# Two transformer layers with routed experts on one core: keys and values from combined weights, a choice of experts on logits, and a written-out end of layer 1

## The chip, the core and the metric

The kernel runs on one core of a Trainium2 chip. A core has separate engines that each work through their own queue of instructions: PE (TensorE, matrix products), DVE (VectorE), ACT (ScalarE), POOL (GpSimd) and SP (SyncE, which here only starts transfers). They wait for one another by semaphores. The metric is the device time of one execution in microseconds (us), and the median of the runs is what is compared. A traced execution gives the time of every instruction; the trace's span runs from its first to its last recorded event.

## The reference

The input is `x` of 8 x 1024 tokens of 128 numbers. All is float32. Four blocks follow, each added to its input, each behind a layer norm:

```python
# layer 0, attention: 8 heads of 32, keys and values through 64 numbers
q = (x @ Wq.T).reshape(b, t, 8, 32)
kv_latent = x @ Wkv_down.T                      # [64]
k = (kv_latent @ Wk_up.T).reshape(b, t, 8, 32)
v = (kv_latent @ Wv_up.T).reshape(b, t, 8, 32)
attn = softmax(einsum('bqhd,bkhd->bhqk', q, k) * 32 ** -0.5)
out = einsum('bhqk,bkhd->bqhd', attn, v).reshape(b, t, 256) @ Wo.T
# layer 0, experts: 2 of 14, F = 256
probs = softmax(x @ gate_w.T)
top2_p, top2_i = top_k(probs, 2)
w = top2_p / maximum(top2_p.sum(-1), 1e-10)
... = w[:, 0] * expert(top2_i[:, 0]) + w[:, 1] * expert(top2_i[:, 1])
# layer 1, linear attention: 16 heads of 8, running sums over the sequence
out = q @ cumsum(k v) / (q @ cumsum(k) + 1e-6) @ Wo.T
# layer 1, experts: 1 of 8, F = 512; above 1280 tokens an expert
# keeps the likeliest, the others go to expert 0
final_e = route(tokens, router_w)
y = relu(tokens @ W1[e] + b1[e]) @ W2[e] + b2[e]
```

## The kernel before

**Attention of layer 0.** Work goes by blocks: one group of four heads and 512 queries. A block has 16 steps (`HALVES`), and the variable `h` counts the steps of all 32 blocks. In a step, `scores` (L398) makes scores of 128 keys against 512 queries for two heads, with ACT's exponential. `smax_step` (L634) makes the largest scores of a block that lies `LEAD` = 24 steps ahead, `weigh` (L413) multiplies earlier exponentials by values (`num`) or by ones (`den`), and POOL adds exponentials in pairs so that `den` needs half the products. The instructions of PE, DVE and ACT go out in the order in which the code writes them (a manual schedule). For POOL and SP, `pinned` calls keep their order.

Other work is put between the steps by hand: `at(h, f)` puts a piece into step `h`. `prepare(b)` (L692) does so with what batch `b` needs in its 64 steps: layer norm, transposes, two `latent` steps (L327, 64 numbers for each token), `project` (L346) for queries and keys, `values` (L335). For batch 0 this is done ahead of the first step (L640 to L658). `complete(b)` (L708) places what follows a batch: output projection, layer norm, and the eleven pieces of `Finish.choice` (L619), the choice of two experts. `last_half` does so for half of batch 7, and the other half comes behind the last block (L790 to L816). In the last 24 steps nothing lies ahead; the code calls them quiet, and there DVE makes the pair sums.

`Finish.choice` makes logits (PE), the maximum and differences (DVE), exponentials (ACT), sum, reciprocal and product (DVE); then twice a maximum, an equality, an index (`candidates`, `choose`). `count` and `rank` give every token its place in its expert's region of the DRAM table `rows_in`, `places` (L593) turns this into addresses. `moving` collects scatters: indirect transfers, issued by POOL, of one row for each of 128 tokens. In the attention loop one goes out every fourth step, in the quiet steps one each step.

**Experts of layer 0.** `expert_tables` (L149) makes, from the counts of tokens per expert, two tables for the tiles of 256 rows: where a tile starts (`row_j`) and which expert it has (`exp_j`). SP reads `row_j` value by value (L200) to fetch tiles; each is transposed, multiplied by two weight matrices and written to `rows_out`.

**Layer 1.** Its loop (L1468) runs over `t`, the pairs of 128-token groups: 32 pairs, four per batch, and three more turns to empty the pipeline. A turn works on several pairs at different stages: gathers of the experts' rows (POOL), `combine` and `stats` for pair t+3, projections for t+1, scores for t, `within` and `turned` for t-1, `project_out` for t-2, and `offset`, `back_norm`, `back_transposed` (layer norm ahead of the experts) for t-3. `stats` (L1026) ends with a power on POOL (`rs`). POOL's gathers, powers and scatters stand in one queue. Two scatters of an earlier batch's rows go out per turn. The pieces of `Route` (L1286), the choice of one expert, are put into slots of later turns by `planned` (L1426). Batch 7 is routed in two halves of four groups: the first from turn 32, the second in turn 34. A `Route` is made like a choice of layer 0, with one expert.

**Experts of layer 1.** `expert_tables` again makes the table, in a pool `d_tab`, then `tiles1` (L1518) runs 36 tiles; SP fetches them from the DRAM table `rows1`, and POOL writes finished rows to `out`. Further tiles and `dropped` run only where experts are overfull.

Of the kernel before, what the change touches and what calls it, by code (L numbers as in the profile page):

```python
# [16 lines left out]
P = 128  # L17
NB = 8
# [34 lines left out]
NOT_AN_EXPERT = 1000.0  # L53
# [24 lines left out]
def tile_two_layers(  # L78
# [36 lines left out]
    def probabilities(b, w_sb, ne, psum, ptag):  # L115

        lg = psum.tile([P, CPB, ne], F32, name="lg", tag=ptag)
        for c in range(CPB):
            nc.tensor.matmul(
                lg[:, c, :], lhsT=xT[b][:, c * P:(c + 1) * P], rhs=w_sb, start=True, stop=True  # L120
            )
        shape = [P, CPB, ne]
        mx = stat.tile([P, CPB], F32, name="mx")
        nc.vector.tensor_reduce(mx, lg, AX.X, ALU.max)
        pr = stat.tile(shape, F32, name="pr", tag=f"pr{ne}")
        nc.vector.tensor_tensor(pr, lg, mx.unsqueeze(2).to_broadcast(shape), ALU.subtract)
        nc.scalar.activation(pr, pr, AF.Exp)
        sm = stat.tile([P, CPB], F32, name="sm")
        nc.vector.tensor_reduce(sm, pr, AX.X, ALU.add)
        nc.vector.reciprocal(sm, sm)  # L130
        nc.vector.tensor_tensor(pr, pr, sm.unsqueeze(2).to_broadcast(shape), ALU.mult)
        return pr

    def first_of_largest(pr, ne, indices, oh, fi):


        shape = [P, CPB, ne]
        pm = stat.tile([P, CPB], F32, name="pm")
        nc.vector.tensor_reduce(pm, pr, AX.X, ALU.max)
        cand = stat.tile(shape, F32, name="cand", tag=f"cand{ne}")  # L140
        nc.vector.tensor_tensor(cand, pr, pm.unsqueeze(2).to_broadcast(shape), ALU.is_equal)
        nc.vector.scalar_tensor_tensor(
            cand, cand, -NOT_AN_EXPERT, indices.unsqueeze(1).to_broadcast(shape), ALU.mult, ALU.add
        )
        nc.vector.tensor_reduce(fi, cand, AX.X, ALU.min)
        nc.vector.tensor_tensor(oh, cand, fi.unsqueeze(2).to_broadcast(shape), ALU.is_equal)
        return pm

    def expert_tables(tab, psum, ptag, counts, ne, nt):  # L149
# [21 lines left out]
        ej = tab.tile([1, nt], F32, name="ej")  # L171
        nc.vector.tensor_reduce(ej, past, AX.X, ALU.add)
        nc.vector.tensor_scalar(ej, ej, float(ne - 1), None, ALU.min)
        exp_j = tab.tile([1, nt], mybir.dt.int32, name="exp_j")
        nc.vector.tensor_copy(exp_j, ej)
# [8 lines left out]
        nc.vector.tensor_tensor(past, past, hop[0:1].unsqueeze(1).to_broadcast(jshape), ALU.mult)  # L184
        rj = tab.tile([1, nt], F32, name="rj")
        nc.vector.tensor_reduce(rj, past, AX.X, ALU.add)
# [3 lines left out]
        nc.vector.tensor_copy(row_j, rj)  # L190
        return SimpleNamespace(exp_j=exp_j, row_j=row_j, base=base, tot=tot, upto=upto)
# [35 lines left out]
    with ExitStack() as ph:  # L227
# [14 lines left out]
        wkd_sb = wts.tile([P, R0], F32, name="wkd_sb")  # L242
# [12 lines left out]
        nc.gpsimd.memset(ones_h, 1.0)  # L255
        def load_rest():
# [17 lines left out]
        kvls, vs, outs = {}, {}, {}  # L274
# [52 lines left out]
        def latent(b, h):  # L327
            ps = bank(name="lat")
            cols = slice(h * BLK, (h + 1) * BLK)
            if h == 0:  # L330
                kvls[b] = work.tile([R0, T], F32, name="kvl", bufs=1)
            nc.tensor.matmul(ps[:R0, :], lhsT=wkd_sb, rhs=xT[b][:, cols], start=True, stop=True)
            nc.scalar.copy(kvls[b][:, cols], ps[:R0, :])

        def values(b, c2):  # L335
            ps = bank((P, 2, 8 * HD0), "val")
            if c2 == 0:
                vs[b] = work.tile([P, CPB, 8 * HD0], F32, name="v")
            for i in range(2):
                c = 2 * c2 + i  # L340
                nc.tensor.matmul(
                    ps[:, i, :], lhsT=kvls[b][:, c * P:(c + 1) * P], rhs=wvu_sb, start=True, stop=True
                )
            nc.scalar.copy(vs[b][:, 2 * c2:2 * c2 + 2, :], ps)

        def project(n, of_k, h):  # L346

            b, g = divmod(n, 2)
            if n not in kTs:
                qTs[n] = work.tile([P, T], F32, name="qT", bufs=3)  # L350
                kTs[n] = work.tile([P, T], F32, name="kT", bufs=3)
            dst, w, src = (kTs, wku_sb, kvls) if of_k else (qTs, wq_sb, xT)
            cols = slice(h * BLK, (h + 1) * BLK)
            ps = bank(name="prj")
            nc.tensor.matmul(ps, lhsT=w[:, g * P:(g + 1) * P], rhs=src[b][:, cols], start=True, stop=True)
            nc.scalar.copy(dst[n][:, cols], ps)
# [103 lines left out]
        class Finish:  # L460
# [46 lines left out]
            def exponentials(self):  # L507
                nc.scalar.activation(self.pr, self.pr, AF.Exp)

            def softmax(self):  # L510
                sm = self.tile("sm", [P, self.n])
                nc.vector.tensor_reduce(sm, self.pr, AX.X, ALU.add)
                nc.vector.reciprocal(sm, sm)
                nc.vector.tensor_tensor(
                    self.pr, self.pr, sm.unsqueeze(2).to_broadcast(self.shape), ALU.mult
                )

            def candidates(self, pr):
                pm = self.tile("pm", [P, self.n], bufs=4)
                nc.vector.tensor_reduce(pm, pr, AX.X, ALU.max)  # L520
                cand = self.tile("cand")
                nc.vector.tensor_tensor(cand, pr, pm.unsqueeze(2).to_broadcast(self.shape), ALU.is_equal)
                nc.vector.scalar_tensor_tensor(
                    cand, cand, -NOT_AN_EXPERT,
                    cst[:, C_I14:C_I14 + E0].unsqueeze(1).to_broadcast(self.shape), ALU.mult, ALU.add,
                )
                return pm, cand
# [8 lines left out]
            def first(self):  # L536
                self.p1, self.cand = self.candidates(self.pr)

            def second(self):
                self.oh1 = self.choose(0, self.cand)  # L540
                rest = self.tile("rest", bufs=1)
                nc.vector.scalar_tensor_tensor(rest, self.oh1, -2.0, self.pr, ALU.mult, ALU.add)
                self.rest = rest

            def third(self):
                self.p2, self.cand = self.candidates(self.rest)

            def fourth(self):
                self.oh2 = self.choose(1, self.cand)

# [42 lines left out]
            def places(self):  # L593

                n, b, c0 = self.n, self.b, self.c0
                at = stat0.tile([P, 2, CPB], U32, name="at")
                for k in range(2):
# [4 lines left out]
                        to, chosen[:, k, b, c0:c0 + n], float(REG0), mine, ALU.mult, ALU.add  # L602
                    )
                    nc.vector.tensor_scalar(at[:, k, :n], to, float(TW0), None, ALU.add)
                xn = self.xn

                def move(j, k):
                    ins = nc.gpsimd.indirect_dma_start(  # L608
                        out=rows_in, out_offset=bass.IndirectOffsetOnAxis(ap=at[:, k, j:j + 1], axis=0),
# [7 lines left out]
                moving.extend(lambda j=j, k=k: move(j, k) for j in range(n) for k in range(2))  # L617

            def choice(self):  # L619
                return [  # L620
                    self.logits, self.exponentials, self.softmax, self.first, self.second, self.third,
                    self.fourth, self.count, self.rank, self.places, self.weights,
# [19 lines left out]
        norms = [Norm(0, c0, CPK, xn, xT[0]) for c0 in (0, CPK)]  # L642
        for f in norms:
# [7 lines left out]
        for h in range(2):  # L651
            latent(0, h)
# [39 lines left out]
        def prepare(b):  # L692
# [4 lines left out]
            for i, h in enumerate((17, 20)):  # L697
                at(h0 + h, latent, b, i)
            for (of_k, i), h in zip(((True, 0), (False, 0), (True, 1), (False, 1)), (24, 25, 28, 29)):
# [8 lines left out]
        def complete(b):  # L708
# [6 lines left out]
            hs = (36, 37, 38, 42, 46, 50, 54, 58, 60, 62, 66)  # L715
            if b == NB - 2:
                hs = (33, 34, 34, 38, 40, 41, 42, 42, 43, 44, 45)
# [3 lines left out]
        def last_half():  # L721
# [5 lines left out]
            for h, piece in zip((51, 52, 53, 54, 55, 56, 57, 57, 58, 59, 60), f.choice()):  # L727
# [12 lines left out]
        for n, qb in blocks:  # L740
            for kc in range(CPB):
                for hp in range(2):
# [24 lines left out]
                    if kc % 2 == 1 and hp == 1:  # L767
                        for i in range(4):
                            if not quiet:
                                pinned(nc.gpsimd.tensor_tensor, first[:, i, :], first[:, i, :], e[:, i, :], ALU.add)  # L770
                            else:
# [18 lines left out]
        n, qb = blocks[-1]  # L790
        weigh(*weighing, den=False)
        weigh(*summing, den=True)
# [83 lines left out]
    with ExitStack() as ph:  # L876
# [60 lines left out]
        def places():  # L937
# [3 lines left out]
            for b in range(0, NB, NB // 2):  # L941
                for k in range(2):
# [4 lines left out]
                        pick, of_expert, cst[:, C_J:C_J + E0].unsqueeze(1).to_broadcast(shape), ALU.is_equal  # L947
# [55 lines left out]
    with ExitStack() as ph:  # L1003
# [22 lines left out]
        def stats(p):  # L1026
# [10 lines left out]
            tc.keep_in_program_order(nc.gpsimd.tensor_tensor(rs, ve, mhalf[:, :PAIR], ALU.pow))  # L1037
# [16 lines left out]

        products = []

        def behind_within(ins):

            if products:
                tc.add_manual_dep(  # L1060
                    ins, products.pop(),
                    mybir.DependencyInfo(mybir.DependencyClass.Sync, mybir.DependencyReason.DATA),
                    reason="the order of issue",
                )
# [221 lines left out]
        class Route:  # L1286
# [23 lines left out]
            def exponentials(self):  # L1310
                nc.scalar.activation(self.pr, self.pr, AF.Exp)

            def softmax(self):
                sm = self.tile("sm1", [P, self.n])
                nc.vector.tensor_reduce(sm, self.pr, AX.X, ALU.add)
                nc.vector.reciprocal(sm, sm)
                nc.vector.tensor_tensor(
# [497 lines left out]
```

## Time and profile before

| | us |
|---|---|
| median of 3 runs | 2088.29 (2085.06 to 2090.93) |
| the profiled execution | 2075.58 |
| its span | 2073.8 |

The span falls into stages. The table gives the busy time of three engines in each, and the clock that the throttle granted to TensorE as a share of full speed:

| stretch, us | what | PE | DVE | POOL | clock |
|---|---|---|---|---|---|
| 0 to 20 | loading, batch 0 | 9.38 | 3.80 | 5.28 | 1.00 |
| 20 to 1305 | attention, layer 0 | 1269.10 | 935.75 | 820.91 | 0.99 |
| 1305 to 1336 | last choice, table | 5.25 | 17.97 | 13.51 | 0.50 |
| 1336 to 1490 | experts of layer 0 | 153.79 | 100.75 | 48.09 | 0.98 |
| 1490 to 1525 | first gathers | 9.06 | 10.76 | 22.33 | 0.56 |
| 1525 to 1877 | layer 1, full turns | 351.18 | 250.54 | 193.19 | 0.92 |
| 1877 to 1923 | layer 1, last turns, table | 13.24 | 17.97 | 21.73 | 0.61 |
| 1923 to 2074 | experts of layer 1 | 136.79 | 69.79 | 79.33 | 0.95 |

A line of the profile gives the source line, the engine, and the operation with its result and operands by their names in the program (`num<-e,v`), partitions x elements, and then times. "PE L332 MATMUL lat<-xT,wkd_sb" is the latent's product in L332. A line that begins with an engine's name and "q" is that engine's queue control. Matmuls are pipelined: in the timeline a matmul's end is modelled, so the distance from one start to the next is what a step holds PE.

### The profile page before, as it was taken

The page shows a single profiled execution, that of the slowest core. Times are in us where ns is not written, and L with a number is a line of the kernel's source. Part 1 is how long each engine was busy: PE and PEld are TensorE (multiplying, and loading weights), DVE is VectorE, ACT ScalarE, POOL GpSimd, SP SyncE. Part 2 cuts the span into 40 slices and gives each one's busy share as a digit, 9 for nine tenths or more (in the row PEclk, how much of TensorE's full clock was granted, in tenths as well). Part 3 has the DMA queues.
Part 4 walks back from the last instruction along what each step waited for, and adds up shares of the span by engine and source line. Part 5 has one row for each costly group of instructions (what it writes and reads, how often), then busy time and mean ns, then how long its engine had stood idle before and what let it go on. Part 6 is the DMA issues. An engine that isn't in the chain of part 4 may idle for free. (4 is left out here: it accounts for less than half of the span.)

```text
span 2073.8 us, 45378 instructions
## 1 busy us (share of the span) xinstructions
PE 1947.8 (94%) x17426; PEld 1005.2 (48%) x17426; DVE 1407.3 (68%) x3614; ACT 1121.2 (54%) x2356; POOL 1204.4 (58%) x1320
## 2 busy tenths in 40 slices
PE   7999999999999999999999997499779999994997
PEld 3333333333333333333333333399747777773896
DVE  6767768758768768768767776567547787764453
ACT  2655555555565565565565455166447766661443
POOL 1556656657667667667666775423355576634455
PEclk9999999999999999999999999699959999995999
DMA  6000000000000000000000000144323311111331
GB/s 225 1 2 2 1 2 3 8 7 9 8 8 9 8 8 10 8 8 8 9 7 8 15 8 26 46 140 137 101 59 85 94 53 49 48 34 52 105 105 58
DMA packets 49872, 81.58 MB, mean 39 GB/s; under 512 B 13498, under 2 KB 32449, under 8 KB 49521
## 3 DMA queue, kind: packets, MB, share of 16 engines
q0 software_dynamic: 17808, 41.55, 6.1%
q1 hardware_dynamic: 28384, 29.10, 4.9%
q10 hardware_dynamic: 3456, 7.95, 1.2%
q8 instruction: 140, 2.29, 0.5%
q14 instruction: 84, 0.68, 0.1%
HBM read 42.73 MB, written 35.96 MB: 38 GB/s over the span
## 5 line engine op out<-in xcount | busy, mean ns | idle before, releaser
L370 DVE TENSOR_REDUCE nmp<-big 128x1 f32<-128x512 f32 x1000 | 642.0, 682 | 295.3 <-PE st L406 259.3
L409 ACT ACTIVATE e<-st 128x512 f32<-128x512 f32 x1000 | 544.3, 595 | 467.6 <-PE st L406 398.8
L240 POOL TENSOR_TENSOR e<-e 128x512 f32<-128x512 f32 x488 | 603.4, 1265 | 50.0 <-PE num L423 50.0
L366 PE MATMUL big<-kT,qT 32*128 32x512 f32 x2000 | 630.4, 641 | 0.2 <-DVE nmp L370 0.2
L406 PE MATMUL st<-qT,kT 32*128 32x512 f32 x2000 | 530.0, 589 | 0.0
L423 PE MATMUL num<-e,v 128*32 128x512 f32 x3064 | 300.7, 465 | 8.5 <-ACT nums L451 8.5
L240 POOL TENSOR_TENSOR outT<-nums,dens 128x64 f32<-128x64 f32 x248 | 79.1, 320 | 376.4 <-DVE dens L441 275.0
L406 PEld LDWEIGHTS st<-qT,kT 32*128 32x128 f32 x2000 | 212.7, 191 | 2.9 <-issue 1.2
L405 PE MATMUL st<-nb,ones_h 3*128 3x512 bf16 x1000 | 210.5, 385 | 1.3 <-DVE nmp L370 1.3
L405 PEld LDWEIGHTS <-ones_h 3*128 3x128 bf16 x1024 | 51.1, 91 | 320.5 <-issue 314.5
L423 PEld LDWEIGHTS num<-e,v 128*32 128x32 f32 x3064 | 61.3, 108 | 296.9 <-issue 264.6
L366 PEld LDWEIGHTS big<-kT,qT 32*128 32x128 f32 x2000 | 194.6, 183 | 21.9 <-DVE nmp L370 17.9
L1072 POOL DMA_INDIRECT got<-rows_out,found x128 | 126.0, 984 | 97.1 <-PE tp L1107 44.9
L608 POOL DMA_INDIRECT rows_in<-xn,at x128 | 132.1, 1032 | 45.2 <-issue 32.8
L441 DVE RECIPROCAL dens<-dens 128x64 f32<-128x64 f32 x248 | 129.9, 536 | 17.1 <-ACT dens L436 17.0
L423 PE MATMUL den<-e,ones 128*32 128x512 f32 x1024 | 141.0, 608 | 0.2 <-POOL e L240 0.2
L1585 POOL DMA_INDIRECT out_x<-y,to x72 | 79.3, 1102 | 74.7 <-DVE y L1583 58.0
L1566 ACT ACTIVATE g<-ph,wt 128x256 f32<-128x256 f32 x144 | 63.8, 474 | 92.6 <-PE ph L1563 92.6
L933 POOL DMA_DIRECT2D rows_out<-y x77 | 44.5, 578 | 106.9 <-DVE y L932 99.7
L923 PEld LDWEIGHTS py<-wt,g 128*128 128x128 f32 x616 | 80.8, 192 | 3.9
L1037 POOL TENSOR_TENSOR rs<-ve,mhalf 128x2 f32<-128x2 f32 x64 | 46.4, 726 | 62.0 <-DVE ve L1035 53.5
L923 PE MATMUL py<-wt,g 128*128 128x128 f32 x616 | 81.0, 275 | 0.0
(284 smaller groups left out, 2989.1 us busy)
## 6 DMA issues: line engine op xcount, KB each, us to landing
xr<-rows_in SPq DMA_DIRECT2D x77, 128.0 KB
rows_out<-y POOLq DMA_DIRECT2D x77, 128.0 KB, 2.3
xr<-rows SPq DMA_DIRECT2D x36, 257.0 KB
nb<-part SPq DMA_DIRECT2D x384, 1.0 KB
blob<-in_blob ACTq DMA_DIRECT2D x8, 578.0 KB
blob<-in_blob SPq DMA_DIRECT2D x1, 4494.0 KB
x<-in_x SPq DMA_DIRECT2D x8, 512.0 KB
rows<-nil ACTq DMA_DIRECT2D x9, 257.0 KB
```

The costliest lines, as they stand in the source:

```text
L240: return tc.keep_in_program_order(f(*args, **kw))
L366: nc.tensor.matmul(ps, lhsT=qTs[n][r, qc * P:(qc + 1) * P], rhs=kTs[n][r, kb * BLK:(kb + 1) * BLK], start=True, stop=True,)
L370: nc.vector.tensor_reduce(nmps[n][:, h, qc, kb:kb + 1], ps, AX.X, ALU.max, negate=True)
L405: nc.tensor.matmul(st, lhsT=ones_h[r3, :], rhs=nbs[n][r3, cols], start=True, stop=False)
L406: nc.tensor.matmul(st, lhsT=kTs[n][r, kc * P:(kc + 1) * P], rhs=qTs[n][r, cols], start=False, stop=True)
L409: nc.scalar.activation(e[:, h, :], st, AF.Exp, scale=SCALE0)
L423: nc.tensor.matmul(vds[key][32 * h:32 * h + 32, cols], lhsT=ones[:, :HD0] if den else vs[b][:, kc, c0:c0 + HD0], rhs=e[:, h, cols], start= ...
L441: nc.vector.reciprocal(s[:, cols], s[:, cols])
L608: ins = nc.gpsimd.indirect_dma_start(out=rows_in, out_offset=bass.IndirectOffsetOnAxis(ap=at[:, k, j:j + 1], axis=0), in_=xn[:, c0 + j, :] ...
L923: nc.tensor.matmul(ps[:, i, :], lhsT=g[:, k, i * P:(i + 1) * P], rhs=w[:, B_W2 + k * D:B_W2 + (k + 1) * D], start=k == 0, stop=k == K0 - 1,)
L1072: ins = tc.keep_in_program_order(nc.gpsimd.indirect_dma_start(out=gots[p][:, i, k, :], out_offset=None, in_=rows_out, in_offset=bass.Indir ...
L1585: ins = nc.gpsimd.indirect_dma_start(out=out_rows, out_offset=bass.IndirectOffsetOnAxis(ap=at[:, i:i + 1], axis=0), in_=y[:, i, :], in_off ...
```

## The change

The change has these parts.

1. Keys and values of layer 0 come straight from the normalised tokens. Two products at the start (`combined_weights`) multiply the down projection by each up projection, two ACT copies put the results into `wk_sb` and `wv_sb`; `latent` is gone, `project` for keys and `values` contract 128 numbers in place of 64. Their places among the steps move four steps forward in `prepare` for the first head group. `wkd` is loaded in its other orientation.
2. The choice in layer 0 works on logits less their maximum: the largest is where this is 0. `first` follows `logits` at once, the exponential goes into its own tile `ex`, the second choice is made on the differences too, and the softmax is reduced to the two probabilities that are needed (`exponential2`, `softmax`), placed behind `places`. Indices are scaled by 1/`UNIT` so that one operation compares and inserts the index. Each of the two address sets has its own tile, and all scatters of first choices come before those of second choices.
3. In layer 0's last block the last pair sums on DVE are dropped; `den` takes the two tiles one after the other.
4. `expert_tables` makes `row_j` ahead of `exp_j`.
5. `Route` in layer 1 is made in the same way as the choice in layer 0: `choose` needs the differences alone.
6. Two scatters per slot go out in layer 1's turns once the gathers have ended, and five at the end of turn 31. The powers issued then stand behind the scatters before them (`since`, `behind`). The route of batch 6 is a turn earlier.
7. The last three turns of layer 1 are written out in a new order.
8. The pool `d_tab` gets `reuse_waits="tile"`: its tiles wait for what last used their own memory and not for all of the pools before. The table's code is in a manual schedule for PE and DVE.

```diff
-        def latent(b, h):
-            ps = bank(name="lat")
...
-            nc.tensor.matmul(ps[:R0, :], lhsT=wkd_sb, rhs=xT[b][:, cols], start=True, stop=True)
-            nc.scalar.copy(kvls[b][:, cols], ps[:R0, :])
+        def combined_weights():
+            ps = bank((P, 2, 8 * HD0), "lat")
+            for i, w in enumerate((wku_sb, wvu_sb)):
+                nc.tensor.matmul(ps[:, i, :], lhsT=wkd_sb, rhs=w, start=True, stop=True)
+            nc.scalar.copy(wk_sb, ps[:, 0, :])
+            nc.scalar.copy(wv_sb, ps[:, 1, :])
...
-                    ps[:, i, :], lhsT=kvls[b][:, c * P:(c + 1) * P], rhs=wvu_sb, start=True, stop=True
+                    ps[:, i, :], lhsT=xT[b][:, c * P:(c + 1) * P], rhs=wv_sb, start=True, stop=True
...
-            dst, w, src = (kTs, wku_sb, kvls) if of_k else (qTs, wq_sb, xT)
+            dst, w = (kTs, wk_sb) if of_k else (qTs, wq_sb)
...
             def first(self):
-                self.p1, self.cand = self.candidates(self.pr)
+                cand = self.tile("cand")
+                nc.vector.scalar_tensor_tensor(cand, self.pr, 0.0, self.indices(), ALU.is_lt, ALU.max)
+                self.oh1 = self.choose(0, cand)
 
             def second(self):
-                self.oh1 = self.choose(0, self.cand)
                 rest = self.tile("rest", bufs=1)
-                nc.vector.scalar_tensor_tensor(rest, self.oh1, -2.0, self.pr, ALU.mult, ALU.add)
+                nc.vector.scalar_tensor_tensor(rest, self.oh1, -LOW, self.pr, ALU.mult, ALU.add)
+                self.top2 = self.tile("top2", [P, self.n])
+                nc.vector.tensor_reduce(self.top2, rest, AX.X, ALU.max)
                 self.rest = rest
 
             def third(self):
-                self.p2, self.cand = self.candidates(self.rest)
+                cand = self.tile("cand")
+                nc.vector.tensor_tensor(
+                    cand, self.rest, self.top2.unsqueeze(2).to_broadcast(self.shape), ALU.is_lt
+                )
+                nc.vector.tensor_tensor(cand, cand, self.indices(), ALU.max)
+                self.cand = cand
...
+            def exponential2(self):
+                self.e2 = self.tile("e2", [P, self.n])
+                nc.scalar.activation(self.e2, self.top2, AF.Exp)
+
+            def softmax(self):
+                self.p1, self.p2 = (self.tile(name, [P, self.n]) for name in ("p1", "p2"))
+                nc.vector.tensor_reduce(self.p1, self.ex, AX.X, ALU.add)
+                nc.vector.reciprocal(self.p1, self.p1)
+                nc.vector.tensor_tensor(self.p2, self.e2, self.p1, ALU.mult)
...
-                moving.extend(lambda j=j, k=k: move(j, k) for j in range(n) for k in range(2))
+                moving.extend(lambda j=j, k=k: move(j, k) for k in range(2) for j in range(n))
...
                 return [
-                    self.logits, self.exponentials, self.softmax, self.first, self.second, self.third,
-                    self.fourth, self.count, self.rank, self.places, self.weights,
+                    self.logits, self.first, self.exponentials, self.second, self.third, self.fourth,
+                    self.exponential2, self.count, self.rank, self.places, self.softmax, self.weights,
                 ]
...
+        combined_weights()
         for f in norms:
...
-        for h in range(2):
-            latent(0, h)
         for of_k, h in ((False, 0), (True, 0), (True, 1)):
...
-            for i, h in enumerate((17, 20)):
-                at(h0 + h, latent, b, i)
-            for (of_k, i), h in zip(((True, 0), (False, 0), (True, 1), (False, 1)), (24, 25, 28, 29)):
+            for (of_k, i), h in zip(((True, 0), (False, 0), (True, 1), (False, 1)), (20, 21, 24, 25)):
                 at(h0 + h, project, 2 * b, of_k, i)
...
-            hs = (36, 37, 38, 42, 46, 50, 54, 58, 60, 62, 66)
+            hs = (36, 38, 37, 42, 46, 50, 47, 54, 56, 58, 62, 66)
             if b == NB - 2:
-                hs = (33, 34, 34, 38, 40, 41, 42, 42, 43, 44, 45)
+                hs = (33, 34, 34, 38, 39, 40, 40, 41, 42, 43, 44, 45)
...
-                            else:
+                            elif h < STEPS - 1:
                                 nc.vector.tensor_tensor(first[:, i, :], first[:, i, :], e[:, i, :], ALU.add)
...
+        weigh(n, qb, CPB - 2, first, den=True)
+        weigh(*weighing, den=True)
         weigh(*weighing, den=False)
-        weigh(*summing, den=True)
...
-            tc.keep_in_program_order(nc.gpsimd.tensor_tensor(rs, ve, mhalf[:, :PAIR], ALU.pow))
+            ins = tc.keep_in_program_order(nc.gpsimd.tensor_tensor(rs, ve, mhalf[:, :PAIR], ALU.pow)).ins
+            if gathered[0] == PAIR * NPAIR:
+                for name in since:
+                    behind(ins, name)
+            since.clear()
...
+                nc.vector.scalar_tensor_tensor(
+                    cand, self.pr, 0.0, cst[:, C_I8:C_I8 + E1].unsqueeze(1).to_broadcast(self.shape),
+                    ALU.is_lt, ALU.max,
+                )
...
-        for t in range(NPAIR + 3):
+        for t in range(NPAIR):
...
-            scatter(1)
+            scattered = 1 if 12 + 2 * t < PAIR * NPAIR else 2
+            scatter(scattered)
...
+            if t == NPAIR - 1:
+                scatter(5)
...
+        p = NPAIR - 1
+        within(p)
+        att_transposed(p - 1)
+        offset(p - 2)
+        back_norm(p - 2)
+        scatter(3)
+        turned(p)
+        divide(p)
+        project_out(p - 1)
+        back_transposed(p - 2)
+        stats(p - 1)
+        att_transposed(p)
+        project_out(p)
+        stats(p)
+        offset(p - 1)
+        back_norm(p - 1)
+        first, second = (Route(NB - 1, c0, CPB // 2) for c0 in (0, CPB // 2))
+        first.logits()
+        first.choose()
+        first.exponentials()
+        offset(p)
+        back_norm(p)
+        back_transposed(p - 1)
+        first.count()
+        back_transposed(p)
+        first.rank()
+        second.logits()
+        first.places()
+        scatter(4)
+        first.softmax()
+        first.keep_top()
+        second.choose()
+        second.exponentials()
+        second.count()
+        second.rank()
+        second.places()
+        scatter(4)
+        second.softmax()
+        assert not moving
+        second.keep_top()
...
-        tab = ph.enter_context(tc.tile_pool(name="d_tab", bufs=1))
+        tab = ph.enter_context(tc.tile_pool(name="d_tab", bufs=1, reuse_waits="tile"))
...
-                tables.__dict__.update(expert_tables(tab, px, "px", counts1, E1, NT1).__dict__)
+                with tc.manual_schedule(engines={mybir.EngineType.PE, mybir.EngineType.DVE}):
+                    tables.__dict__.update(expert_tables(tab, px, "px", counts1, E1, NT1).__dict__)
...
```

## The prediction

> **What bounds the kernel.** I read the page's shares first, then busy time by stage, the PE timeline inside a stage, and last the chain of waits.
>
> ```profile
> PE 1947.8 (94%) x17426; PEld 1005.2 (48%) x17426; DVE 1407.3 (68%) x3614; ACT 1121.2 (54%) x2356; POOL 1204.4 (58%) x1320
> ```
>
> TensorE leads, but this averages stages. In the windows view (PE, PEld, DVE, ACT, POOL busy; clock; DMA) the long attention stage has PE full and everything else with room; around 1870 to 1950 nothing is full.
>
> ```profile
> 140.00:200.00 60.00, 60.00 (x498) 19.89 (x500) 44.62 (x83) 31.38 (x58) 37.37 (x42) 1.00 0.01 2
> 1870.00:1900.00 30.00, 18.68 (x200) 15.43 (x200) 13.90 (x68) 5.65 (x16) 14.21 (x16) 0.67 0.15 53
> 1900.00:1950.00 50.00, 28.11 (x173) 25.56 (x173) 20.57 (x71) 12.75 (x29) 18.23 (x18) 0.72 0.28 89
> ```
>
> So each PE step taken out of attention is worth its issue time; at the joints between stages the latency of a chain counts. PE's timeline around what the change removes and widens (start, length):
>
> ```profile
> 88.84 0.64 PE L423 MATMUL num<-e,v 128*32 128x256 f32 x8
> 89.41 1.07 PE L332 MATMUL lat<-xT,wkd_sb 128*64 128x512 f32 x2
> 90.41 0.40 PE L405 MATMUL st<-nb,ones_h 3*128 3x512 bf16 x2
> ...
> 105.64 1.12 PE L355 MATMUL prj<-kvl,wku_sb 64*128 64x512 f32 x2
> 106.70 0.39 PE L405 MATMUL st<-nb,ones_h 3*128 3x512 bf16 x2
> ...
> 108.82 1.12 PE L355 MATMUL prj<-xT,wq_sb 128*128 128x512 f32 x2
> 109.88 0.40 PE L405 MATMUL st<-nb,ones_h 3*128 3x512 bf16 x2
> ```
>
> A latent step holds PE from 89.41 to 90.41, 1.00 us. A projection over 64 rows and one over 128 both hold it 1.06.
>
> Last, the chain that ended last, from the last scatter to the first expert tile of layer 1:
>
> ```profile
> 1909.55 2.64 DMA rows<-row,where
> 1912.22 0.05 DVEq L157
> 1912.31 0.42 DVE grid L157
> ...
> 1918.31 0.18 DVE row_j L190
> 1918.61 0.72 SPq L200
> 1919.33 0.07 issue
> 1920.04 2.82 DMA xr<-rows
> 1922.90 0.70 PE px L1554 x2
> ```
>
> The expert table (grid to row_j, 6.2 us) starts only when the last scatter has landed.
>
> **1. Latents, steady part.** Two per batch for batches 1 to 7: 14 x 1.00 = **14.0 us**. K and V now contract 128 rows. A rule speaks against this. The row says 1.06 us for either height, so widening costs 0. TensorEngine Tiling (Array Packing), Overview, says a contraction of at most 64 rows can share the array, up to 2x. If the 64-row steps had shared it, their widening would cost up to 0.53 us for each of some 28 key and 28 value steps in the steady part, 30 us. I take the row: the next matmul starts 1.06 after the 64-row one, so nothing shared it. Fewer PE microseconds could expose another engine: DVE has 26% and POOL 38% free in 140 to 200. Ends 13 and 15.
>
> **2. Prologue.** Before: two latents (12.77 to 16.4, cold, 1.8 each), prj q 16.38, prj k 17.44, kT copied 18.60 to 19.19, first scores 19.35. After: q and k follow the transposes at 12.84. Row: four cold latent matmuls took 3.68 us, four warm prj matmuls 1.98. TensorE: Matmul & The Clock Gate, Part 1, says warm-up is about 3.4 us of sustained time, not a count of matmuls; so q and k inherit the cold stretch. Warm, they would end at 15.0 and scores start at 15.7 (3.6 won). Cold, 1.8 each: 16.5, copy, scores at 17.2: **2.2 us**. Added: two weight products, ahead of the transposes on PE, and two copies (some 0.35 each) ahead of the first xn on ACT. Behind them wait all of batch 0's transposes. ACT loads its table until 7.95 and starts xn at 9.01, which holds both copies if wvu lands by about 8. Ahead of it: x0, cst and small weights, 1.24 MB; the windows view shows 1.2 MB moved by 6 us. If x1 shares the engines it is nearer 8. Were wvu as late as 13.4 (when SP's issue that waits for its semaphore starts), 4 us would be lost. Ends -2 and 3.6.
>
> **3. Quiet end of attention.** PE stood here for 8.5 us:
>
> ```profile
> 1267.77 1.04 POOL L240 TENSOR_TENSOR rs<-ve,mhalf 128x4 f32<-128x4 f32 x1
> ```
>
> PE's num waits for ACT's nums copy, behind xn, behind off, behind this power, which stands behind 11 scatters (1254.16 to 1267.75, 1.26 each). All shift with their addresses. Six operations leave the choice ahead of them, two come (the second maximum and one comparison, about 0.27 each), and count and rank come a step earlier, so rk (1249.69, idle 1.33 for `both`) holds PE less: I estimate addresses 1.9 us earlier, and 1.1 more from the same at 1288.84 (1.68 idle). **3.0 us**, ends 0 and 5. The new ACT exponential of top2 stands where ACT idles 5 us; nothing it hides costs over 0.3.
>
> The last sum in the block falls away: den's last matmul ended near 1299 behind four DVE adds (to 1297.88). Now one more weigh (1.0 us of PE) replaces them, and the reciprocal starts near 1298.1: **1.0 us**, ends 0 and 2.
>
> **4. Joint to the experts of layer 0.** From logits at 1312.92 to first scatter at 1320.72, then eight scatters to 1332.4, landing, fetch. Leaving the path: exponential 0.29, sum 0.24, reciprocal 0.21, product 0.25, maximum 0.25, equality 0.25 = 1.49. Separate address tiles let the first four scatters go after the first address (0.5 earlier). Softmax and weights run under the scatters. **2.0 us**, ends 1 and 3.5. The table, row addresses first, is shorter than the scatters, as it was.
>
> **5. Layer 1, loop.** PE is full there too. DVE loses three operations of 0.22 per batch; PE's waits on it are small. Two scatters per slot come only where gathers have ended: per slot, two scatters (2.5 us) replace two gathers and one (3.8), so the powers ordered behind them aren't late. **0.5 us**, ends -1 and 3.
>
> **6. Layer 1's end.** Before: the last pair's power was ready at 1889.88 and ran at 1895.32, behind eight scatters; first half scattered from 1899.70, second from 1905.73. After: backlog is cleared inside the loop, five scatters in its last turn. The moved rank adds 0.8 of cold PE to that turn, which ends near 1877.4 for 1877.0. Then, with this trace's durations: power of pair 30 at 1884.3 (behind three scatters), of pair 31 at 1886.8; first half's choice, five DVE operations of 0.2, done 1888.0; rows of pair 31 normalised 1889.2; transposes and rank, cold, 1890.9; second half's logits 1892.6, its maximum and difference ahead of the addresses on DVE; addresses 1893.9. Scatters from 1894.3, second half's addresses (1897.9) in time; eight x 1.27 end 1904.5, last landing 1903.2 + 2.64 = 1905.8, against 1912.2. The table's waits are now for old gathers, not scatters (the changed program's instruction order shows it): 6.2 us from about 1898.6, done by 1904.8, SP's lookup 0.72 after. The fetch starts at 1905.8 + 0.7 = 1906.5 instead of 1920.04: **13.5 us**. It is hidden with under a microsecond to spare; any delay beyond that comes out of the gain. Ends 8 and 17 (cold PE; steadier POOL).
>
> **Sum.** 14.0 + 2.2 + 3.0 + 1.0 + 2.0 + 0.5 + 13.5 = 36.2 us. The profiled execution took 2075.58 (span 2073.8 and 1.8 around it): 2039.4, a ratio of 0.9826. The three runs' median is 2088.29, 12.7 above that execution: times 0.9826, **2052 us**.
>
> **Rivals.** (a) Latents were hidden: a PE step less only meets another wait. Against it PE without idle at 60.00 of 60.00. It gives 22 us, 2066. Chance 0.07. (b) The written-out end stalls on in-order queues (second logits ahead of first addresses, cold rank) or the table reaches past the landing, and gives 6 of 13.5: 29 us, 2059. For it: clock 0.67 in this stretch. Chance 0.18. This includes that the table still waits for scatters. (c) Slower: each of the 56 widened steps, K and V of the steady part, loses an overlap with its neighbour. From 0.65 us each (36.2 / 56) it decides; a whole 1.06 each is 59 us: 2039.4 + 59 = 2098, by ratio 2111. Against it 105.64 to 106.70 above. Chance 0.03.
>
> **Numbers.** Forecast 0.72. All ends at once would give gains of 19 to 50; they hardly fall together, so its own range is 2043 to 2061; 2041 to 2066 takes in (b) and nearly all of (a). Faster by over 0.3% (about what a measurement of this kernel tells from no change) 0.95, within it 0.02, slower 0.03.
>
> **What would show it.** No lat; prj and val still 1.06 apart; one batch some 2 us shorter. First scores near 17.2. The power of 1267.77 some 4 us past the latents' gain. First scatter of batch 7 in layer 1 about 5 us nearer to the loop's end; grid no longer waiting for DMA rows; xr issued within 1 us of the last landing. Wrong if widened steps take over 1.06, or row_j ends the wait before xr.

## The result, and the profile after

The changed kernel takes 2083.99 us (median of 20 runs, 2076.89 to 2091.88). The kernel before, in 20 runs beside it, takes 2097.94 (2085.06 to 2115.21). The ratio is 0.9928, with a 95% interval of 0.9907 to 0.9950. The change is faster, by 14 us. 36 us were forecast, and a time between 2041 and 2066.

The profiled execution of the changed kernel took 2081.75 us (span 2080.0), which is more than the 2075.58 of the kernel before. First the page's shares:

```profile
PE 1962.0 (94%) x17406; PEld 1015.8 (49%) x17406; DVE 1390.5 (67%) x3565; ACT 1113.8 (54%) x2351; POOL 1204.4 (58%) x1320
```

There are 20 matmuls fewer, but TensorE is busy for 14 us more (1947.8 before). The windows view says where. Its columns are busy us (x instructions) of PE, PEld, DVE, ACT and POOL, the granted clock, the DMA share and GB/s. First the changed kernel: inside attention, in layer 1 from the first to the last product of `keys_values`, and from there to the first expert tile.

```profile
140.00:200.00 60.00, 60.00 (x500) 19.76 (x492) 44.94 (x83) 31.74 (x60) 37.39 (x42) 1.00 0.01 2
1506.00:1880.00 374.00, 361.32 (x5017) 254.75 (x5017) 240.86 (x927) 224.45 (x578) 196.44 (x215) 0.91 0.18 56
1880.00:1929.00 49.00, 29.21 (x313) 21.99 (x311) 22.45 (x105) 9.66 (x25) 21.63 (x23) 0.61 0.19 65
```

The last two stretches in the first profile of the kernel before:

```profile
1520.40:1862.60 342.20, 341.78 (x5017) 245.93 (x5016) 245.19 (x945) 224.85 (x578) 194.75 (x212) 0.93 0.21 61
1862.60:1922.90 60.30, 27.15 (x313) 20.80 (x311) 23.93 (x113) 9.79 (x25) 23.73 (x25) 0.59 0.17 56
```

The end became shorter, 49 us where it was 60.3, in the direction that was forecast. But the turns of layer 1 take 374 us where they took 342, with the same 5017 matmuls, with less work of DVE and about the same of ACT and POOL. Up to the first `keys_values` the changed kernel was 14.2 us ahead (1506.17 against 1520.35); the turns lose more than twice that.

Then the signs that the prediction named. In attention there is no `lat`, and keys now contract 128 rows (PE's timeline of the changed kernel: start, length):

```profile
105.56 1.13 PE L323 MATMUL prj<-xT,wk_sb 128*128 128x512 f32 x2
106.62 0.39 PE L373 MATMUL st<-nb,ones_h 3*128 3x512 bf16 x2
...
108.74 1.13 PE L323 MATMUL prj<-xT,wq_sb 128*128 128x512 f32 x2
109.80 0.39 PE L373 MATMUL st<-nb,ones_h 3*128 3x512 bf16 x2
```

Both still hold PE for 1.06 us. The chain at the end of layer 1:

```profile
1922.98 2.77 DMA rows<-row,where
1926.37 2.65 DMA xr<-rows
1929.06 0.69 PE px L1568 x2
```

The table no longer stands in it: the fetch starts 0.6 us after the last scatter has landed (7.8 us before). The first scatter of batch 7 starts 34.1 us after the last `keys_values`, for 37.1 before: 3 us nearer, for about 5 forecast.

### The profile page after: what moved, and what is told of

Its sections match the earlier page's. It is cut to its first block, busy times and chain, and to the rows that moved or that the text cites. A ratio compares the mean times of both kernels' runs of the same rounds, so it can differ in the third digit from the quotient of the medians.

```text
span 2080.0 us, 45296 instructions
## 1 busy us (share of the span) xinstructions
PE 1962.0 (94%) x17406; PEld 1015.8 (49%) x17406; DVE 1390.5 (67%) x3565; ACT 1113.8 (54%) x2351; POOL 1204.4 (58%) x1320
## 5 line engine op out<-in xcount | busy, mean ns | idle before, releaser
L373 PEld LDWEIGHTS <-ones_h 3*128 3x128 bf16 x1024 | 51.3, 91 | 314.0 <-issue 307.1
L582 POOL DMA_INDIRECT rows_in<-xn,at x128 | 131.5, 1027 | 38.5 <-issue 30.3
L1109 ACT ACTIVATE qm<-qk,cst 128x256 f32<-128x256 f32 x128 | 54.6, 496 | 52.7 <-DVE qk L1106 38.8
```

What stands on the lines that cost most here:

```text
L373: nc.tensor.matmul(st, lhsT=ones_h[r3, :], rhs=nbs[n][r3, cols], start=True, stop=False)
L582: ins = nc.gpsimd.indirect_dma_start(out=rows_in, out_offset=bass.IndirectOffsetOnAxis(ap=ats[k][:, j:j + 1], axis=0), in_=xn[:, c0 + j, : ...
```

## Experiments

**Where the 32 us in layer 1's turns come from.** Theory 1 says that the change makes the turns slower by itself. Theory 2 says that most executions of either kernel have slow turns, and that the first profile of before fell on a quiet one. Both kernels were profiled again, one execution each, without an edit.

> The kernel before, profiled a second time. Theory 1 (the change makes layer 1's turns slower by itself): layer 1 from the first keys_values product to the last takes 342 us again (within 4), without gaps put down to issue. Theory 2 (layer 1's turns are disturbed in most executions of either kernel, and the first profile of before fell on a quiet one): it takes 355 us or more, with gaps put down to issue and more time at half clock, and the span is above 2083.

Measured: 2109.65 us. First to last `keys_values` took 367.5 us, not 342, with 5.7 us of gaps put down to issue (time in which PE waited for nothing that the profile shows). That is theory 2's number.

> The changed kernel, profiled a second time. Theory 1: layer 1 from the first keys_values product to the last takes 374 us again, and its slow places are the same pairs. Theory 2: it differs by 8 us or more, and the slow places are other pairs. Attention's last scores step within 3 us of 1278.6 by both.

Measured: 2082.63 us and 370.3 us in the turns. Some of the slow pairs are others; the slowest turn is the same, turn 30 with 20.8 us. Neither theory has all of this.

Then each half of the change alone, as the kernel before plus these parts:

- `layer0_only`: parts 1 to 4 of the change (`combined_weights`, `Finish` and the places of its pieces, the last sums, the order of the tables);
- `layer1_only`: parts 5 to 8 (`Route`, the scatters of the turns, `since`, the written-out end, `d_tab`).

> The kernel before with the change's layer 0 alone (combined weights, choice on logits, last sums, table order). Theory 1: about 14 us faster than before (ratio 0.992 to 0.995), that is the whole gain of the change, layer 1's part giving back what its end wins. Theory 2: about the same 14 us, which is half to two thirds of the gain.

Measured: 2083.55 for 2099.30, ratio 0.9935 (0.9910 to 0.9960).

> The kernel before with the change's layer 1 alone (choice on logits, two scatters per slot, written-out end, table's waits). Theory 1: no faster than before (ratio 0.998 to 1.006): 11 us won from the last keys_values to the first expert tile, as much or more lost in the turns. Theory 2: 8 to 13 us faster (ratio 0.994 to 0.996).

Measured: 2100.00 for 2099.30, ratio 1.0007 (0.9985 to 1.0029). Layer 0's part is the whole gain and layer 1's part gives nothing, within the intervals. The trace of `layer1_only` has a shorter end (54.0 us) and 371.7 us in the turns; `before_again` and `layer0_only`, with the old turns, have 367.5 and 357.6. So both theories hold a part: the turns are slow with either kernel, and somewhat slower with the new one.

**What makes TensorE slow there.** Turn 30 of the changed kernel, timeline of PE and POOL (start, length, in brackets idle time ahead):

```profile
1861.04 1.03 POOL L1359 DMA_INDIRECT rows<-row,where  x1 [0.17 <-issue]
...
1861.46 0.69 PE L1189 MATMUL oT<-am,va 128*32 128x64 f32 x33
1862.35 0.32 PE L1189 MATMUL oT<-am,va 128*32 128x64 f32 x4 [0.20 <-issue]
...
1862.38 0.97 POOL L1359 DMA_INDIRECT rows<-row,where  x1 [0.30 <-issue]
...
1863.10 0.31 PE L1189 MATMUL oT<-am,va 128*32 128x64 f32 x4 [0.44 <-issue]
...
1863.65 0.97 POOL L1359 DMA_INDIRECT rows<-row,where  x1 [0.30 <-issue]
1863.86 0.33 PE L1189 MATMUL oT<-am,va 128*32 128x64 f32 x5 [0.44 <-issue]
...
1866.81 0.46 PE L1189 MATMUL oT<-am,va 128*32 128x64 f32 x6 [0.48 <-issue]
```

`within`, 64 short products, runs at once until about the second scatter, and then mostly in handfuls of four to six every 0.75 us. From its first start to its last it takes 5.49 us; without a scatter beside it and outside half clock it takes 0.88. The granted clock is at half for 10.2 us from 1866.7 on. The same spans were measured in all eight traces that show such turns (those so far but the first profile of before, and three that come below), always outside half clock. The `scores1` of one pair take 0.76 us on average where no indirect transfer, gather or scatter, lies beside them (91 cases), and 1.73 where one does (106). For `within` it is 0.88 (209 cases) and 2.26 (9).

Theory A: the indirect transfers do this. Theory B: TensorE's own instruction supply does, whatever is transferred. Theory C: any work of POOL does. Four kernels were run for it. The first two are the changed kernel with

```diff
-            scattered = 1 if 12 + 2 * t < PAIR * NPAIR else 2
+            scattered = 1 if t < 22 else 0
 # and every later scatter behind the second half's places
+            busy(t)     # pool_busy_instead: gpsimd.memset of an unused buffer
```

> The changed kernel with the scatters of batches 3 to 7 put behind the last turn; turns 12 to 21 still scatter, turns 22 to 31 do not. Theory A (TensorE loses time while POOL issues indirect transfers): scores of one pair take 0.74 us and within 0.88 us in turns 22 to 31 outside half clock, against 1.2 to 2.0 and up to 5.5; turns 12 to 21 stay as they are (1.2 to 2.0); first to last keys_values takes about 350 us in place of 370 to 374, with the gaps put down to issue gone from turn 22 on. Theory B (the gaps are TensorE's own instruction supply): the gaps stay in turns 22 to 31, first to last keys_values 365 us or more. The end gets some 40 us longer by both.

> As scatters_deferred, but POOL writes zeros into an unused buffer for about 1.2 us wherever a scatter was left out of turns 22 to 31. Theory A as stated: TensorE is as in scatters_deferred (0.74 and 0.88). Theory C (any work of POOL beside it slows TensorE): scores 1.2 us or more and within over 1.5 us again where the writes overlap them.

The third, `scatter_behind_within`, adds to a scatter in a turn without gathers the wait for the last product of `within`, which gathers have:

```diff
             behind(ins, last.name)
+            if gathered[0] == PAIR * NPAIR:
+                behind_within(ins)
```

> The changed kernel; from turn 26 on, where gathers have ended, the first scatter of a turn waits for the last product of within, as gathers do. Theory A: within of turn 30 falls from 5.5 us to 0.9, of turn 31 from 3.1 to 0.9, less half clock after them; 7 to 12 us faster than the changed kernel, ratio to before 0.987 to 0.991. Theory B: no gain, ratio 0.992 to 0.995.

The fourth is the kernel before with the combined weights alone:

> The kernel before with the combined weights alone (no latent steps, keys and values contract 128 rows). By the prediction's steps 1 and 2 it is 16.2 us faster (ratio 0.992); if 14 latents are worth 0.9 us each and the start gives 0.8, it is 13.4 us (0.9936) and carries the whole gain of layer 0's part; if the choice and the last sums bring what was forecast (6.0 us), it must be 6 us slower than layer0_only, whose ratio is 0.9935.

Measured: scatters_deferred 2076.05, pool_busy_instead 2077.64, scatter_behind_within 2043.23 (0.9859, 0.9833 to 0.9885), weights_only 2056.32 (0.9921, 0.9903 to 0.9939), beside a kernel before of 2072.98, 26 us below its time so far. On this chip the slow products are absent: `scores1` 0.74 and `within` 0.88 to 0.90 in all pairs outside half clock, with scatters or not, and the turns take 338 to 340 us in all four, the old turns of weights_only too. So these runs don't tell A, B and C apart. They show two kinds of behaviour, which fall together with the chip so far; below, "first kind" is a chip without the slow products and "second kind" one with them. The first profile of before shows the first kind, the profile after the second.

> The changed kernel once more, timed. The runs so far fall in two groups by the chip they ran on: where scores of a pair beside a scatter take 0.74 us (the first profile of before; the last four kernels; before at 2073 us) and where they take 1.2 to 2.0 (before at 2099 us). If this chip is of the first kind, theory D (the chip decides what a scatter costs TensorE, and the prediction's sum holds where it costs nothing) expects first to last keys_values of 340 us, ratio 0.983 to 0.987. If it is of the second kind, 370 us and 0.990 to 0.995 again. Theory E (the changed kernel is slower in its turns on any chip) expects 0.990 to 0.995 on either.

Measured, beside a kernel before of 2071.61: the changed kernel 2037.59, ratio **0.9851** (0.9826 to 0.9876), turns of 338 us. That is theory D (the chip decides what a scatter costs TensorE), and E (the changed kernel is slower in its turns on any chip) falls. Its turn 30, the same four scatters at the same place:

```profile
1829.32 1.03 POOL L1359 DMA_INDIRECT rows<-row,where  x1 [0.18 <-issue]
...
1829.74 1.10 PE L1189 MATMUL oT<-am,va 128*32 128x64 f32 x64
1830.65 0.97 POOL L1359 DMA_INDIRECT rows<-row,where  x1 [0.30 <-issue]
...
1830.77 0.44 PE L1239 MATMUL tp<-cst,att 128*128 128x128 f32 x2
```

64 products in one go. The next set, on another chip, gave the same.

> The changed kernel on the same chip, to compare. Second kind: first to last keys_values 370 us, ratio 0.990 to 0.995; first kind: 340 us, 0.985.

Measured: the changed kernel 2037.85 for 2072.87, 0.9850 (0.9818 to 0.9882). The other repeats in these two sets were expected as before: scatters_deferred took 2067.49 and 2070.08 and pool_busy_instead 2071.89, without slow products; scatter_behind_within 2039.95 (0.9853) and 2035.66 (0.9833), the same as the changed kernel within the intervals.

The last set met the second kind again (the kernel before at 2097.04), on a chip that none of these sets had used.

> The scatters of batches 3 to 7 behind the last turn. Second kind: theory A expects scores of 1.2 to 2.0 us in turns 12 to 21 and 0.74 in turns 22 to 31 outside half clock; theory B 1.2 to 2.0 in both. First kind: 0.74 in all.

Measured: 2097.2 us. One pair's scores in turn 20, with a scatter beside, and in turn 24, without:

```profile
1742.77 1.00 POOL L1359 DMA_INDIRECT rows<-row,where  x1 [0.30 <-issue]
...
1742.84 1.36 PE L1168 MATMUL a<-qm,qk 32*64 32x256 f32 x31
...
1744.58 0.41 PE L1168 MATMUL a<-qm,qk 32*64 32x256 f32 x1 [0.37 <-issue]
```

```profile
1788.40 1.12 PE L1168 MATMUL a<-qm,qk 32*64 32x256 f32 x32
```

Scores 12 to 22 take 1.26 to 2.01 us from first start to last where a scatter lies beside them (0.75 in the one pair of these without), scores 23 to 31 take 0.74 and every `within` 0.88, outside half clock. The turns take 351.4 us for some 370. Turns 22 to 30, where the scatters are gone, take 100.5 us together. In the five traces of the second kind that have the new turns they take 113.4 to 119.2, and with the new turns on the first kind 99.5 to 101.0; turn 30 alone takes 11.8, for 20.8 to 22.8 in the five. The turns ahead of them keep their scatters and take 249.7 us, for 252.7 to 254.8 in the five. That is theory A's number, and B falls as it was put: the program that TensorE executes there is the same, only the scatters are gone. The trace's packets of the instruction queue don't speak for B either: between 1500 and 1930 us one takes 1.01 to 1.13 us on average in the eight traces of the second kind and 1.05 to 1.16 in those of the first.

pool_busy_instead, which was to test C, met no chip of the second kind, but the traces at hand bear on it. In turn 30 of the changed kernel POOL makes a power beside the scores, and no transfer is there:

```profile
1859.96 1.12 PE L1168 MATMUL a<-qm,qk 32*64 32x256 f32 x32
1860.17 0.69 POOL L1010 TENSOR_TENSOR rs<-ve,mhalf 128x2 f32<-128x2 f32 x1 [9.88 <-DVE ve L1008]
```

From first start to last these scores take 0.74 us (the 1.12 reaches to the modelled end of the last). So it is in all 34 `scores1` and 96 `within` of the eight traces that have a power and no indirect transfer beside them, outside half clock: 0.74, and 0.88 to 0.93. It is not any work of POOL, then; other work of POOL than this power was not looked at.

> The changed kernel with the first scatter of a turn behind the last product of within. Second kind: theory A expects within of turns 30 and 31 at 0.9 us in place of 5.5 and 3.1 and a ratio of 0.987 to 0.991; theory B 0.992 to 0.995. First kind: 0.983 to 0.987 again.

Measured: 2086.46, ratio 0.9935 (0.9911 to 0.9959), `within` of turn 30 still 5.5 us. The first of turn 30's four scatters starts at 1858.54, before `within` does at 1858.95, and the others run beside it: the wait that the edit was to add does not hold them there. So the cure was not tested where it was needed; this run counts neither for A nor against it.

> The kernel before with the change's layer 1 alone. On a chip of the first kind (before near 2072 us) its turns cost nothing more and the end gives 13 to 16 us: ratio 0.992 to 0.994, against 1.0007 on the second kind. On one of the second kind 0.998 to 1.003 again.

Measured: ratio 1.0012 (0.9986 to 1.0037), 368.9 us in the turns and 48.2 in the end. Layer 1's part again gives nothing on the second kind.

## Why the prediction was wrong, step by step

The prediction's base was a profile of the first kind, and the result was measured on the second. The terms, in us gained, by the trace; "first kind" compares the first profile of before and weights_only with five profiles that have the whole change (after_third, after_fourth and the three of scatter_behind_within); "second kind" compares before_again and layer0_only (old turns) with five that have the new turns (after, after_again, layer1_only, layer1_only_again, behind_within_4).

| step | forecast | first kind | second kind, the result's |
|---|---|---|---|
| 1 latents, the choice in the steps | 14.0 | 14.5 - 3.1 | 11.4 together |
| 2 prologue | 2.2 | 0 | 0 |
| 3 quiet end and last sum | 4.0 | about 3 | about 1 |
| 4 joint | 2.0 | 1.8 | 1.8 |
| 5 turns of layer 1 | 0.5 | 3 | **about -9** |
| 6 end of layer 1 | 13.5 | 15.7 | 9 |
| sum | 36.2 | 35 | 14 |
| measured, medians | | 34.0 and 35.0 | 14.0 |

**Step 5 failed.** It said of the two scatters per slot that they "replace two gathers and one (3.8), so the powers ordered behind them aren't late", and took 0.5 us. It priced a scatter as POOL's time, and as free to TensorE. On the second kind it isn't: the old turns take 367.5 and 357.6 us (mean 362.6), the new ones 373.8, 370.3, 371.7, 368.9 and 374.3 (371.8), and on the first kind both take 336 to 342. So both kernels pay for their transfers there, and the new one pays more. In the new order four scatters follow each other beside `within` of turn 30, where the old one has one or two beside a `within` (1.3 to 2.8 us): this turn takes 20.8 to 22.8 us in all five, 13.6 and 19.3 with the old, which is some 5 of the 9 us, and deferred_4, without these scatters, has 11.8. The rest is spread over the turns and was not followed to a cause; half clock varies there (28.9 and 46.6 us of the old turns, 49.9 to 67.1 of the new). With two old traces 10 us apart the 9 is rough, but the medians need a loss of that size: layer1_only changes nothing, 1.0007 and 1.0012, though its end is about 9 us shorter. The range of this step, -1 to 3, had no place for that.

Step 6 gave 9 of its 13.5 us, and scatters stand at the place of the loss. Its working, where power, ranks and table follow each other, is right on the first kind: 60.3 and 60.2 us shrink to 43.0 to 45.1 in the five. On the second, 63.7 and 56.6 shrink only to 48.2 to 54.2: scatters lie beside `within` of turn 31 or of the written-out end (3.06 and 2.19 us in the changed kernel's profile, 2.99 and 2.62 in layer1_only_again's), and the clock is at half for 30.3 to 44.0 us of the end, for 29.1 to 34.3 on the first kind. What each of the two costs was not measured. Rival (b) let the end give only 6 of 13.5 us, by in-order queues; the place was right, but the same queues lose nothing on the first kind.

**Behind it, the base.** The profile that was read for all of this shows `scores1` at 0.74 us beside scatters, so no row in it held the price:

```profile
1707.72 0.99 POOL L1383 DMA_INDIRECT rows<-row,where  x1 [0.30 <-issue]
1707.85 1.12 PE L1186 MATMUL a<-qm,qk 32*64 32x256 f32 x32
```

One sign was in view: the execution took 2075.58, less than the fastest of the three runs (2085.06), and the prediction carried the 12.7 us to the median over as a ratio. It said how far apart they were, and not that a difference of that size had a place somewhere in the kernel. It was mostly in layer 1's turns: before_again spends 25 us more there. The three runs lie with those of the second kind (2085 to 2120) and outside those of the first (2061 to 2077), so the forecast mixed two kinds of chip.

**Step 1 was right, and the choice cost something it was not charged.** From the first scores step to step 448, executions without half clock take 1090.94 us with the old layer 0 (layer1_only_again) and 1079.52 with the new one (after_third): 11.4. With the combined weights alone it is 1078.76, with 6.8 us at half clock. In after_fourth the same 6.8 us, in the same first half of a batch, cost 2.4, so it would be about 1076.4 without: 14.5 for 14 latents, 1.0 each. The new choice takes about 3.1 of them back. In three half-batches it is 75.23 us with the whole change for 74.70 with the weights alone, and the difference appears where `rank`'s product now stands (1.03 us more in that step, 0.5 given back in those behind). By the medians weights_only is 16.7 us faster than before, where steps 1 and 2 forecast 16.2. That DVE and POOL would not be the bound held. That 64 rows cost as much as 128 held too (1.06): the Trainium skill's TensorEngine Tiling (Array Packing), Overview, which the prediction weighed, says that a contraction of at most 64 rows can run at up to twice the speed by sharing the array; these steps did not. So rival (c) falls, and (a) with the 14.5.

**Step 2 failed in a term.** It said that ACT's start at 9.01 "holds both copies if wvu lands by about 8". In the profile after:

```profile
10.35 0.37 ACT L300 COPY wk_sb<-lat 128x256 f32<-128x256 f32 x1 [2.88 <-PE lat L299]
10.62 0.38 ACT L301 COPY wv_sb<-lat 128x256 f32<-128x256 f32 x1
10.88 0.89 ACT L284 ACTIVATE xn<-x,off,rs 128x128 f32<-128x128 f32 x2
```

The weight products wait for `wku` until 8.27 and for `wvu` until 8.90, the copies for the products until 10.35, and ACT's `xn` starts 1.9 us later than before. The sum had a time for the two copies and none for the two products, which hold PE from 8.27 to 10.32. The first scores start at 18.3 to 19.9 us in the runs with combined weights (19.0 to 19.6 with latents; 17.2 forecast), and the first step of the attention loop when it did before, at 49.9 to 51.3 (50.4 to 51.0).

**Steps 3 and 4 held about.** The power of the quiet end stands at

```profile
1248.49 1.04 POOL L207 TENSOR_TENSOR rs<-ve,mhalf 128x4 f32<-128x4 f32 x1
```

which is 118.2 us after step 448, for 121.3 and 122.9 in the two profiles of before: 3 to 5 us earlier, for 4 forecast. From step 448 to the last logits the first kind takes 166.1 us in the profile of before and 162.2 to 165.2 with the whole change. On the second kind the executions differ by more than the gain (167.6 to 174.8 with the old layer 0, 167.4 to 175.2 with the new), and no run here shows why; this stretch too has scatters, up to eleven behind each other. The joint to the experts of layer 0, from the last product of the logits to the first of a tile, went from 23.46 to 21.6 us, 1.8 of the 2.0. One sum of the prediction is a little off: all its upper ends together give 49.1, not 50, which moves nothing.

## What to carry to other kernels

Before a profile's durations are summed, ask whether that execution is like the runs whose time is to be forecast: one that is 0.5% faster than the fastest of them leaves something out, and where it does so is part of the base. A transfer that an engine issues is not always priced by that engine's time alone; look at what runs beside it at a high rate of short instructions, in several executions, and give its price to the other engine as one end of the range. A gain that depends on where transfers stand should be measured on more than one chip before it is believed: 0.9851 and 0.9928 are both well measured, and are the same change.

## What the runs showed of the hardware

The chips fall in two kinds. On two of them (the kernel before at 2072 to 2073 us), and in the first profile of before, indirect transfers of POOL cost TensorE nothing that a trace shows: 157 `scores1` beside one and 141 without take 0.74 us. On two others (2097 to 2099 us) they take 1.73 and 0.76, and `within` up to 5.5 us for 0.88 (9.3 with six scatters beside it, clock at half). The Trainium skill, SBUF — State Buffer, section "SBUF: two separate sides", says that compute operations and transfers can't slow each other, as their ports are apart. The first kind agrees. On the second products are slower beside the transfers, so the measurement decides there, and the section can't be read as "a transfer is free to TensorE". By which way the transfers reach TensorE, no run here shows. Nor is it shown that the chip itself makes the kind: one chip was met in two sets and was of the same kind in both, the other three in one set each, so something else that holds through a set could do it. After the slow `within` of turn 30 the clock is granted at 0.5 for 10.2 us. The Trainium skill, TensorE: Matmul & The Clock Gate, Part 1, gives half clock after at least one idle window of about 3.4 us; here TensorE was not idle for so long: the longest gap in these 5.5 us is 0.48. In attention the first profile of before has half clock for 10.2 us from 449.9 on, and its trace shows no gap of PE in it or in the 20 us ahead. So idle time is not the only thing that goes before half clock in these traces, and what else brings it is open.

No version here beats the changed kernel beyond the intervals. Keeping the scatters from `within` and `scores1` on chips of the second kind would be the next step: deferred_4 shows 351.4 us in the turns for 370, but its end takes 79.2 us for 48.2 to 54.2, as everything is scattered there.
